# One PSUM bank in halves for sums that begin as a copy, and projection sums handed over one by one

## Chip, cores and metric

The kernel runs on one core of one Trainium2 chip. The metric is the device time of one execution in microseconds (us). The profile is one execution taken by the hardware profiler on the same core. Engines: PE (TensorE), DVE (VectorE), ACT (ScalarE), POOL (GpSimd) and SP (SyncE, which here only issues DMAs).

## The reference

With x of 3327 x 512, a 0/1 matrix adj of 3327 x 3327 (about 1% ones), two weights W of 512 x 1024 and one weight of 512 x 512, all float32:

```
h = x
for W in W_stack:                       # two layers
    Wh, Ws = split(h @ W, 2, axis=-1)   # two of 3327 x 512
    a = softmax(Wh @ Ws.T, axis=-1) * adj
    h = leaky_relu(a @ Wh + h, 0.01)
x = layernorm(x + h)
xw = maximum(sign(x), 0) @ sign(weight).T
return layernorm(x + relu(adj @ xw))
```

## The kernel before

**Tiling.** The 3327 rows are 26 tiles of 128. Four tiles make a chunk (seven chunks c, the last of two tiles), two tiles a pair (13 pairs q as keys, 13 column halves g as queries). A product `A @ B` whose operands split into 2 x 2 blocks is made in seven block products (r 1 to 7) in place of eight, from sums of the blocks; four of these at once (a quad of two pairs q, against both halves g of a chunk) are made in 26 products in place of 28. All of it is float32, 128 x 128 weights against 256 columns; a matmul of this kind shows as two records.

**The projection** (`project`, once per layer) makes Wh for each pair (`project_values`) and the query forms for each chunk (`queries`, names ending in `_g`). Each is a chain of seven products (`seven`, from line 199): three sums Z, Y, X, each in a PSUM bank, where X begins as a copy of Z by ACT (`seeded`) and gets only product 2. The sums of operands that a chain needs (`left_sums`, `right_sums`: `key_sums`, the `sums` of `queries`) and those made from its results (`done`, `last_sums`, and `query_sums` for the blocks' extra forms `ge`) are DVE work; POOL's queue stores the results to DRAM (`xs_d`, `ws_d`, `gs_d`, `ge_d`). `weave` lists the steps of several chains by their relative places, and everything is issued in that order (a manual schedule), so each engine runs its part of one written order.

**The attention** (`attention`, once per layer) goes through 169 steps (g, q): softmax weights times adjacency times Wh, as seven-product chains into the `acc` banks (L1092). Woven into the steps are the scores of the chunk ahead, 26 half-steps u for each chunk, of some 6 us each. A pair q outside the quads gets one chain by `scores`: z1, y5, z6, y3 in the first half-step, z7, x2, z4 in the second (L771), sums Z, Y, X. A quad (four in layer 1, three in layer 2) gets one block by `quad_scores` in four half-steps (L811): 26 products in the order

```
ORDER = (11, 8, 3, 23, 14, 16, 12, 22, 9, 1, 25, 20, 4,
         21, 13, 7, 19, 24, 6, 5, 15, 18, 2, 10, 17, 0)
```

into the sums P, Q, R, S, T. There are 49 blocks. A running sum is read out along the way, by ACT (`keep_as`, L817) or by a DVE addition (`out`, L823); at two places ACT copies a kept value into a bank to go on from there (`seed`, L820): u2 into Q before r19, c30 into P before r17. The work of a half-step is a list of pairs (place, operation), sorted by place.

**Loads.** Query forms of a chunk (`ga`, `gb`; seven forms B11, T1, T2, B22, T3, B21, T4) are loaded on SP's queue by `load_gs` (L748): five of them in half-steps 20 to 24 of the chunk before, the last two (B21, read by x2, and T4, read by z4) in half-step 0 of the chunk itself. Where a chunk has a single buffer for a form, SP waits for the last reader.

**Column maximum.** For the softmax, `column_max` folds each half's running maximum; in `across`, seven copies of 32 partitions by ACT bring the partial maxima together and spread the result.

**PSUM** has eight banks: three in the pool `ps_ch` (tag `ch`: the sums Z, X, Y of chains and P, Q, R, S, T of blocks), four in `ps_acc`, one in `ps_tr`. In the projection the chains of values use `acc`, those of queries `ch`. `copied` (L885) keeps u2 and p5 of a chain.

Of the kernel before, what the change touches and what calls it, by code (L numbers as in the profile page):

```python
# [19 lines left out]
P = 128  # L20
# [25 lines left out]
def kernel(  # L46
# [39 lines left out]
    ps_ch = ctx.enter_context(tc.tile_pool(name="ps_ch", bufs=3, space=PSUM))  # L86
# [10 lines left out]
    with tc.manual_schedule():  # L97
        make_identity(nc, ident)
        drum = keep.tile([P, HW], BF16, name="drum")
        nc.vector.memset(drum, 0.0)  # L100

        def beat(lane, times):
            pool, tag = lane
            t = pool.tile([P, HW], F32, tag=tag, name="beat")
            for _ in range(times):
                nc.tensor.matmul(t, drum[:, :P], drum, start=True, stop=True)

        for n in range(3):
            beat((ps_ch, "ch"), 2)
        for n in range(4):  # L110
            beat((ps_acc, "acc"), 2 - n % 2)
# [92 lines left out]
    def seven(lane, name, multiply, c11, c12, c21, c22):  # L204
# [19 lines left out]
        def seeded():  # L224
            bank["X"] = pool.tile([P, HW], F32, tag=tag, name=f"pX_{name}")
            nc.scalar.copy(bank["X"], bank["Z"])
# [15 lines left out]
    def left_sums(a11, a12, a21, a22, s1, s2, s3, s4, eng=nc.vector, between=lambda: None):  # L242
        eng.tensor_tensor(s1, a21, a22, ALU.add)
        eng.tensor_tensor(s2, s1, a11, ALU.subtract)
        between()
        eng.tensor_tensor(s3, a11, a21, ALU.subtract)
        eng.tensor_tensor(s4, a12, s2, ALU.subtract)

    def right_sums(b11, b12, b21, b22, t1, t2, t3, t4):
        nc.vector.tensor_tensor(t1, b12, b11, ALU.subtract)  # L250
        nc.vector.tensor_tensor(t2, b22, t1, ALU.subtract)
        nc.vector.tensor_tensor(t3, b22, b12, ALU.subtract)
        nc.vector.tensor_tensor(t4, b21, t2, ALU.subtract)

    def weave(*lists):

        at = [
            ((i + 0.5) / len(part), n, do)
            for n, part in enumerate(lists) for i, do in enumerate(part)
        ]  # L260
        for _, _, do in sorted(at, key=lambda e: e[:2]):
            do()
# [12 lines left out]
    def key_sums(l, q, a, xT, between=lambda: None):  # L275
# [9 lines left out]
        left_sums(  # L285
            *(of[i] for i in (A11, A12, A21, A22, S1, S2, S3, S4)), between=between
        )
        return of
# [74 lines left out]
    def query_sums(l, c, gs, b12):  # L363
# [12 lines left out]
        def first():  # L376
            sub(23, gs[B11][:, 0], gs[T3][:, 1])
            sub(22, gs[B21][:, 1], gs[T4][:, 0])
            sub(2, gs[T3][:, 1], b12[:, 0])
            sub(5, at[22], gs[B22][:, 1])  # L380
            sub(3, at[22], gs[T3][:, 0])
            store(0, 4)

        def second():
            sub(7, gs[B22][:, 0], gs[T1][:, 1])
            sub(13, at[7], gs[B21][:, 0])
            sub(21, at[23], gs[T4][:, 1])
            sub(20, at[7], gs[B11][:, 1])
            sub(9, at[21], at[13])
            store(1, 2, 3)  # L390

        return [first, second]
# [70 lines left out]
    def project(l, pre):  # L463
# [32 lines left out]

        def transpose_x(c, a):
            if a == 0:
                xTs[c] = pre.tile([P, KD, CW], F32, tag="xT", bufs=2, name=f"xT_{l}_{c}")
# [5 lines left out]
        else:  # L505
            xTs[0] = x_first[l]
            for n in range(3):
                beat(ch_lane, 1)
# [28 lines left out]
        def keys(c, a, between=lambda: None):  # L537

            q = c * CT // 2 + a
            of = keys_first.pop((l, q), None) or key_sums(l, q, a, xTs[c], between)  # L540
            if q // 2 in QUADS[l]:
                return of
            to = xs_d[l][q]
            for raw in (A11, A12, A22):
                nc.gpsimd.dma_start(out=to[:, raw], in_=of[raw])
            nc.gpsimd.dma_start(out=to[:, S1 : S2 + 1], in_=of["s12"])
            nc.gpsimd.dma_start(out=to[:, S4 : S3 + 1], in_=of["s34"])
            return of

        def project_values(c, a, lane, between=lambda: None):  # L550
# [12 lines left out]
            def done():  # L563
                t12 = slot([P, 2, HD], F32, f"t12_{l}_{q}")
                t34 = slot([P, 2, HD], F32, f"t34_{l}_{q}")
                right_sums(b11, b12, b21, b22, t12[:, 0], t12[:, 1], t34[:, 0], t34[:, 1])
                nc.gpsimd.dma_start(out=ws_d[l][q][:, 0:2], in_=t12)
                nc.gpsimd.dma_start(out=ws_d[l][q][:, 2:4], in_=t34)

            of_pair[q] = of  # L570
            return (
                [lambda: of.update(keys(c, a, between))]
                + seven(lane, f"wh_{l}_{q}", multiply, b11, b12, b21, b22) + [done]
            )

        def queries(c, lanes):
# [15 lines left out]
            if len(halves_of(c)) == 1:  # L592
# [9 lines left out]
                def last_sums():  # L602
                    store(B11, B21, B22)
                    right_sums(gs[B11], lo[:, :, P:], *(gs[i] for i in (B21, B22, T1, T2, T3, T4)))
                    store(T1, T2, T3, T4)

                more = query_sums(l, c, gs, lo[:, :, P:])
                return None, [lambda e=e: one(e) for e in range(KD)] + [last_sums] + more, []
# [7 lines left out]
            def sums():  # L616
                right_sums(xr[B11], lo[:, :, HW:], *(xr[i] for i in (B21, B22, T1, T2, T3, T4)))
# [10 lines left out]
            def done():  # L628
                store(B11, B21, B22)
                right_sums(gs[B11], b12, *(gs[i] for i in (B21, B22, T1, T2, T3, T4)))  # L630
                store(T1, T2, T3, T4)

# [5 lines left out]
            more_of[c] = [done] + query_sums(l, c, gs, b12)  # L638
            return sums, one, two

        def sums_m():
            of = left(*m_of[l])
            left_sums(
                *(of[i] for i in (A11, A12, A21, A22, S1, S2, S3, S4)),
                eng=nc.gpsimd if l else nc.vector,
            )
# [6 lines left out]
        def prepare(c):  # L653
            start, *chains[c] = queries(c, (ch_lane, ch_lane if c else acc_lane))
            if start:
                start()

        if l == 0:

            first = project_values(0, 0, ch_lane, lambda: (parts[0](), parts[1]()))  # L660
            second = project_values(0, 1, ch_lane)
            first.pop(0)()
            for do in parts[2:]:
                do()
            turns = [lambda k=k: transpose_w(l, 0, k, tr_lane) for k in range(KD)]
            turns.insert(2, lambda: transpose_first(acc_lane, 1))
            turns += [second.pop(0), lambda: None]
            turns += [lambda k=k: transpose_w(l, 1, k, tr_lane) for k in range(KD)]
            for do in first + second[:3]:
                do()  # L670
                turns.pop(0)()
            second = second[3:]
            for do in turns:
                do()
            weave(product_m(l, acc_lane), second, [lambda: prepare(0)])
            sums_m()
        else:
            first, second = (
                project_values(0, a, lane) for a, lane in enumerate((ch_lane, acc_lane))
            )  # L680
            sums_m()
            weave(first, second, [lambda: prepare(0)])
        for c in range(NC):
            turns = []
            if c + 1 < NC:
                turns = [
                    lambda a=a: transpose_x(c + 1, a) for a in range(len(tiles_of(c + 1)))
                ]
                pairs_of[c + 1] = [
                    project_values(c + 1, a, acc_lane)  # L690
                    for a in range(2 if c + 1 in QUADS[l] else 1)
                ]
                turns += [part.pop(0) for part in pairs_of[c + 1]]
                turns += [lambda: prepare(c + 1)]
            turns = rest + turns
            rest = more_of.pop(c, [])
# [4 lines left out]
            else:  # L701
                one, two = chains[c]
                pairs = sum(pairs_of[c], [])
                for a in range(len(pairs_of[c]), len(tiles_of(c)) // 2):
                    pairs += project_values(c, a, acc_lane)
                rest.append(pairs.pop())
                quad = []
                if c in QUADS[l]:
                    quad = quad_sums(l, c, of_pair[2 * c], of_pair[2 * c + 1])
                weave(one + two, pairs, turns, quad)  # L710
        for do in rest:
            do()
# [10 lines left out]
    def attention(l, att):  # L723
# [52 lines left out]
        def quad_scores(c, i):  # L776
# [14 lines left out]
            def fresh(n):  # L791
# [3 lines left out]
            begins = {11: "P", 8: "Q", 3: "R", 24: "S", 10: "T"}  # L795
            joins = dict(zip(
                (23, 12, 1, 4, 7, 6, 18, 17, 14, 22, 25, 21, 19, 5, 2, 16, 9, 20, 13, 15, 0),
                "PPPPPPPPQQQQQQQRRRRST",
            ))

# [32 lines left out]
            for r, b, name, other in (  # L833
                (16, "R", "c10", "c10"), (12, "P", "c31", "c31"), (9, "R", "c11", "c11"),
                (21, "Q", "c10", "c10"), (7, "P", "c00", "c00"), (24, "S", "u3", "u3"),
                (6, "P", "c01", "c01"), (5, "Q", "c01", "c01"), (15, "S", "c20", "c20"),
                (18, "P", "c21", "c21"), (2, "Q", "c11", "c11"), (10, "T", "c21", "c21"),
                (17, "P", "c30", "u3"), (0, "T", "c31", "c31"),
# [5 lines left out]
                (2.42, lambda: seed("Q", "u2")),  # L844
                (3.65, lambda: seed("P", "c30")),
# [23 lines left out]
        def scores(c, q, s):  # L869
# [17 lines left out]
            def z1():  # L887
                product(c, q, "Z", A11, B11, True)
                ch["X"] = ps_ch.tile([P, w], F32, tag="ch", name=f"pX_{l}_{c}_{q}")
# [45 lines left out]
        def column_max(g):  # L935
# [18 lines left out]
            def across():  # L954
                for a in range(P // B):
                    nc.scalar.copy(quad[:B, a], part[ts(a, B)])
# [3 lines left out]
                for a in range(1, P // B):  # L960
                    nc.scalar.copy(whole[ts(a, B)], whole[:B])
# [264 lines left out]
        else:  # L1226
# [35 lines left out]
            def keys_of_first(a):  # L1262
                keys_first[l + 1, a] = key_sums(l + 1, a, a, x_first[l + 1])
# [23 lines left out]
        for v in range(-LOOK - 4, len(steps)):  # L1287
# [18 lines left out]
            if 0 < c < NC and i == 0:  # L1306
                load_gs(c, 5, 2)
            if 0 <= c < NC and 1 <= i < 6:
                load_ge(c, i - 1)
            work, after = after, []  # L1310
            if 0 <= v + 3 < len(steps):
# [82 lines left out]
    def aggregate(g, p, a, e):  # L1394

        if (p, a, e) == (0, 0, 0):
            pool, tag = tr_lane if g == 3 else ch_lane
# [278 lines left out]
```

## Time and profile before

| | |
|---|---|
| median of 3 runs | 2548.84 us (2544.43 to 2550.69) |
| profiled execution | 2545.21 us, span 2543.4 us |
| granted PE clock | 0.998 |
| busy: PE, DVE, POOL, ACT | 2487.9, 2024.7, 1432.6, 859.0 us |
| chain that ended last, by engine | PE 84%, DVE 8%, DMA 4%, issue 2% |
| value products (L1092), four groups | 402.3, 376.4, 376.3, 201.2 us |
| DMA | 652.15 MB, 256 GB/s over the span |

The span is the time from the first to the last recorded instruction. Layer 1 ends near 1223 us; the projections lie at about 30 to 190 and 1230 to 1395 us, the last part (aggregation) follows layer 2. Matmuls are pipelined, so a busy PE is not a PE at its peak, and a matmul's lateness is best read from the distance of starts. "x2" at the end of a timeline row is the number of records in it.

### The profile page before, as it was taken

How to read it: one execution, taken by the hardware profiler on the slowest of the kernel's cores; microseconds unless marked ns; L12 is line 12 of the kernel's file. 1: busy time of each engine (PE TensorE's matmuls, PEld its weight loads, DVE VectorE, ACT ScalarE, POOL GpSimd, SP SyncE). 2: the span in 40 equal slices, each digit the busy share in tenths (PEclk: the TensorE clock that was granted, in tenths of full speed). 3: DMA queues.
4: the chain of work that ended last, by engine and by line, in shares of the span. 5: the costliest groups of instructions: out<-in, count | busy, mean ns of one | idle time of the engine just before them, and what ended most of it. 6: DMA issues, size and time to landing. Idle time of an engine off the chain costs nothing.

```text
span 2543.4 us, 39247 instructions
## 1 busy us (share of the span) xinstructions
PE 2487.9 (98%) x12056; PEld 2137.9 (84%) x12056; DVE 2024.7 (80%) x4020; ACT 859.0 (34%) x2171; POOL 1432.6 (56%) x2452
## 2 busy tenths in 40 slices
PE   9999999999999999999999999999999999999998
PEld 7886888888888888888888788888888888888886
DVE  6976787888878888778897668788787887878876
ACT  3323433323333333322232343332323323332234
POOL 3873465666666665545586345566555665555531
PEclk9999999999999999999999999999999999999999
DMA  5876867777677776798778686877777777788985
GB/s 187 282 286 217 276 229 261 246 259 262 228 269 243 251 267 233 264 312 261 231 275 299 239 282 224 276 241 268 260 227 275 242 266 254 235 271 291 313 279 174
DMA packets 313957, 652.15 MB, mean 256 GB/s; under 512 B 35373, under 2 KB 170661, under 8 KB 313742
## 3 DMA queue, kind: packets, MB, share of 16 engines
q1 hardware_dynamic: 279022, 539.75, 63.4%
q0 software_dynamic: 34720, 109.84, 11.6%
q8 instruction: 98, 1.61, 0.3%
q14 instruction: 117, 0.96, 0.1%
HBM read 539.15 MB, written 110.29 MB: 255 GB/s over the span
## 4 chain that ended last, share of the span: by engine, by line
PE 84%; DVE 8%; DMA 4%; issue 2%; SPq 1%; ACT 1%; POOL 0%; DVEq 0%; ACTq 0%; POOLq 0%
PE acc L1092 36%; PE pZ L771 9%; PE pP L811 6%; PE pQ L811 6%; PE pY L771 4%; PE pR L811 4%; PE agg L1404 3%; DMA ga<-gs_d 3%; PE pX L771 3%; PE pZ_wh L558 2%; PE pZ_g L622 2%; PE pT L811 2%; PE pS L811 2%; DVE ge L370 1%; PE pY_wh L558 1%
## 5 line engine op out<-in xcount | busy, mean ns | idle before, releaser
L1065 POOL TENSOR_TENSOR as<-s 128x128 f32<-128x128 f32 x338 | 204.8, 606 | 675.5 <-DVE s L1032 555.7
L1092 PE MATMUL acc<-ws,s 128*128 128x256 f32 x1352 | 402.3, 379 | 0.0
L1022 ACT ACTIVATE s<-s 128x512 f32<-128x512 f32 x338 | 213.3, 631 | 506.4 <-DVE s L1016 505.4
L1092 PE MATMUL acc<-ws,as 128*128 128x256 f32 x1352 | 376.4, 379 | 0.0
L1092 PE MATMUL acc<-wh,s 128*128 128x256 f32 x1352 | 376.3, 379 | 0.0
L1045 POOL TENSOR_TENSOR deg<-deg,adj 128x256 fp8e4<-128x256 fp8e4 x338 | 248.4, 735 | 62.0 <-DMA adj<-in_adjT_dram 47.7
L1092 PEld LDWEIGHTS acc<-ws,as 128*128 128x128 f32 x1352 | 249.4, 190 | 35.3 <-issue 3.8
L1092 PEld LDWEIGHTS acc<-wh,s 128*128 128x128 f32 x1352 | 250.6, 190 | 32.6
L1092 PEld LDWEIGHTS acc<-ws,s 128*128 128x128 f32 x1352 | 250.8, 190 | 30.8
L1032 DVE TENSOR_TENSOR s<-s,adj 128x512 f32<-128x512 f32 x338 | 242.9, 719 | 9.2 <-DMA adj<-in_adjT_dram 3.4
L867 DVE TENSOR_TENSOR top<-top,s 128x512 f32<-128x512 f32 x286 | 230.4, 807 | 16.1 <-ACT s L918 13.6
L1027 DVE TENSOR_TENSOR total<-total,s 128x512 f32<-128x512 f32 x312 | 243.2, 779 | 0.0
L1016 DVE TENSOR_TENSOR s<-s,beside 128x512 f32<-128x512 f32 x338 | 228.6, 676 | 13.1 <-ACT beside L1011 13.0
L771 PE MATMUL pZ<-ga,xs 128*128 128x256 f32 (+1 forms) x912 | 213.2, 358 | 3.2 <-DVE s L910 2.6
L1066 POOL TENSOR_TENSOR s<-s 128x128 f32<-128x128 f32 x338 | 198.3, 587 | 27.0
L1092 PE MATMUL acc<-wh,as 128*128 128x256 f32 x676 | 201.2, 379 | 0.0
L1067 POOL TENSOR_TENSOR as<-s 128x128 f32<-128x128 f32 x338 | 185.4, 549 | 26.5
L1068 POOL TENSOR_TENSOR as<-s,as 128x128 f32<-128x128 f32 x338 | 180.1, 533 | 26.5
L771 PEld LDWEIGHTS pZ<-ga,xs 128*128 128x128 f32 x912 | 165.2, 190 | 26.5 <-DVE s L910 4.3
L817 ACT COPY s<-pP 128x256 f32<-128x256 f32 (+1 forms) x196 | 70.0, 357 | 248.9 <-PE pP L811 194.2
L811 PE MATMUL pP<-ga,xs 128*128 128x256 f32 (+1 forms) x518 | 144.9, 361 | 3.6 <-DMA xs<-xq_d 2.7
L1092 PEld LDWEIGHTS acc<-wh,as 128*128 128x128 f32 x676 | 123.1, 190 | 19.1 <-issue 3.3
(271 smaller groups left out, 4947.5 us busy)
## 6 DMA issues: line engine op xcount, KB each, us to landing
ws<-ws_d SPq DMA_DIRECT2D x338, 512.0 KB
adj<-in_adjT_dram SPq DMA_DIRECT2D x351, 256.0 KB
xs<-xq_d SPq DMA_DIRECT2D x98, 832.0 KB
xs<-xs_d SPq DMA_DIRECT2D x84, 512.0 KB
xs<-xs_d SPq DMA_DIRECT2D x84, 384.0 KB
gs_d<-gsp POOLq DMA_DIRECT2D x84, 256.0 KB, 4.6
ge_d<-ge POOLq DMA_DIRECT2D x60, 256.0 KB, 3.0
ga<-gs_d SPq DMA_DIRECT2D x54, 256.0 KB
```

The costliest lines, as they stand in the source:

```text
L771: nc.tensor.matmul(ch[bank], xs[c, q, a][:, k], query(c, b)[:, k], start=(start and k == 0), stop=(k == 1), skip_group_check=True,)
L811: nc.tensor.matmul(bank[b], xs[c, i, f"x{r}"], right, start=r in begins, stop=True, skip_group_check=True,)
L867: nc.vector.tensor_tensor(top[i], top[i], t, ALU.max)
L1016: nc.vector.tensor_tensor(s, s, at.to_broadcast([P, 2, HW]), ALU.subtract)
L1022: nc.scalar.activation(sc[g, q], sc[g, q], AF.Exp)
L1027: nc.vector.tensor_tensor(total[g], total[g], sc[g, q], ALU.add)
L1032: nc.vector.tensor_tensor(s, s, adj[g, q], ALU.mult)
L1045: nc.gpsimd.tensor_tensor(deg[:, g], deg[:, g], adj[g, q][:, a], ALU.add, saturate=False)
L1065: nc.gpsimd.tensor_tensor(s3, a11, a21, ALU.subtract)
L1066: nc.gpsimd.tensor_tensor(a21, a21, a22, ALU.add)
L1067: nc.gpsimd.tensor_tensor(s2, a21, a11, ALU.subtract)
L1092: nc.tensor.matmul(acc[g][i // 2][:, i % 2], a[i], b[i], start=(q == 0 and i % 2 == 0), stop=(q == NQ - 1), skip_group_check=True,)
```

## The change

- PSUM: `ps_ch` gets two banks in place of three. The third becomes a bank of its own, `side`, one tile of two halves of 256 columns, for the sums that begin as a copy or as zeros. The X sum of a chain in the projection goes to half 0 for chains of `ch_lane` and to half 1 for the others; X of a chain of scores goes to half q mod 2.
- Blocks: R goes to half 0 and is set to zero by DVE at the start of the block; it begins with r3 as before. What went on in Q from u2 (r19, r5, r2) becomes U in half 1, seeded at place 1.75 in place of 2.42. What went on in P from c30 (r17) becomes V in half 0, seeded at 2.7 in place of 3.65. P, Q, S, T use the two banks of `ps_ch`.
- Projection: the groups of four sums are handed to `weave` as single operations, with the stores between them; the sums after the last chain of a chunk go over into the next chunk's lists, those after its first chain get places of their own (0.53 and on, by 0.09).
- The loads of B21 and T4 of a chunk are issued in half-step 25 of the chunk before, at 0.43 and 0.8.
- In `across`, the copies for the first two halves g are made by DVE.
- Three warm-up matmuls at the start of layer 2 go, and one of the last part's sums uses `side`'s bank.

The diff, cut to its core:

```diff
-    ps_ch = ctx.enter_context(tc.tile_pool(name="ps_ch", bufs=3, space=PSUM))
+    ps_ch = ctx.enter_context(tc.tile_pool(name="ps_ch", bufs=2, space=PSUM))
+    ps_x = ctx.enter_context(tc.tile_pool(name="ps_x", bufs=1, space=PSUM))
...
+        side = ps_x.tile([P, 2, HW], F32, tag="x", name="side")
...
         def seeded():
-            bank["X"] = pool.tile([P, HW], F32, tag=tag, name=f"pX_{name}")
+            bank["X"] = side[:, 0 if lane == ch_lane else 1]
             nc.scalar.copy(bank["X"], bank["Z"])
...
+    def sums_by(eng, *of):
+        return [
+            lambda to=to, a=a, b=b, op=op: eng.tensor_tensor(to, a, b, op) for to, a, b, op in of
+        ]
...
     def weave(*lists):
         at = [
-            ((i + 0.5) / len(part), n, do)
+            ((i + 0.5) / len(part), n, do) if callable(do) else (do[0], n, do[1])
             for n, part in enumerate(lists) for i, do in enumerate(part)
         ]
...
-                rest.append(pairs.pop())
-                quad = []
+                pairs = pairs_of[c]
+                quad, sums = [], []
                 if c in QUADS[l]:
                     quad = quad_sums(l, c, of_pair[2 * c], of_pair[2 * c + 1])
-                weave(one + two, pairs, turns, quad)
+                if len(pairs) == 2:
+                    sums = [(0.53 + 0.09 * n, do) for n, do in enumerate(pairs[0][2])]
+                rest = pairs[-1][2] + rest
+                weave(one + two, sum((part[1] for part in pairs), []), turns, quad, sums)
...
-            begins = {11: "P", 8: "Q", 3: "R", 24: "S", 10: "T"}
+            begins = {11: "P", 8: "Q", 24: "S", 10: "T"}
             joins = dict(zip(
-                (23, 12, 1, 4, 7, 6, 18, 17, 14, 22, 25, 21, 19, 5, 2, 16, 9, 20, 13, 15, 0),
-                "PPPPPPPPQQQQQQQRRRRST",
+                (23, 12, 1, 4, 7, 6, 18, 14, 22, 25, 21, 3, 16, 9, 20, 13, 19, 5, 2, 17, 15, 0),
+                "PPPPPPPQQQQRRRRRUUUVST",
             ))
+            bank.update({n: side[:, e, :w] for n, e in (("R", 0), ("V", 0), ("U", 1))})
...
-                (2.42, lambda: seed("Q", "u2")),
-                (3.65, lambda: seed("P", "c30")),
+                (0.0, lambda: nc.vector.memset(bank["R"], 0.0)),
+                (1.75, lambda: seed("U", "u2")),
+                (2.7, lambda: seed("V", "c30")),
...
             def z1():
                 product(c, q, "Z", A11, B11, True)
-                ch["X"] = ps_ch.tile([P, w], F32, tag="ch", name=f"pX_{l}_{c}_{q}")
+                ch["X"] = side[:, q % 2, :w]
                 nc.scalar.copy(ch["X"], ch["Z"])
...
             def across():
+                copy = nc.vector.tensor_copy if g < 2 else nc.scalar.copy
                 for a in range(P // B):
-                    nc.scalar.copy(quad[:B, a], part[ts(a, B)])
+                    copy(quad[:B, a], part[ts(a, B)])
...
-            if 0 < c < NC and i == 0:
-                load_gs(c, 5, 2)
...
+            if 0 <= c < NC - 1 and i == 2 * NQ - 1:
+                work += [
+                    (at, lambda c=c, n=n: load_gs(c + 1, n)) for n, at in ((5, 0.43), (6, 0.8))
+                ]
```

## The prediction

> **What bounds the kernel now.** I read the page's busy shares first, then the waits of TensorE (PE), then the timelines around the places that the change touches, then the windows of the projection.
>
> ```profile
> PE 2487.9 (98%) x12056; PEld 2137.9 (84%) x12056; DVE 2024.7 (80%) x4020; ACT 859.0 (34%) x2171; POOL 1432.6 (56%) x2452
> ```
>
> PE is the bound: all that can be won is what PE idles, all that can be lost is a new wait of PE, which takes its work in program order. The matmul count does not change (three warm-up beats, 0.3 us, go). Start to start, records follow each other at 0.216 us (128x256); summed over the timeline, PE's starts are some 72 us late against that pace. Columns: waited for, us in total, times, longest.
>
> ```profile
> PE pX L771 <- DMA ga<-gs_d: 7.4, 9, 1.7
> PE pZ_wh L558 <- DVE wh L222: 6.7, 7, 2.2
> PE pQ L811 <- ACT pQ L820: 4.7, 10, 1.6
> PE pZ L771 <- ACT u L885: 3.9, 4, 1.7
> PE pZ_g L622 <- DVE gsp L222: 2.6, 3, 0.9
> PE pS L811 <- DVE qu L823: 2.3, 5, 0.8
> ```
>
> Below, for how soon PE can follow a ScalarE (ACT) seed: the last column's brackets hold idle time and its releaser.
>
> ```profile
> 1841.40 0.37 ACT L817 COPY s<-pP 128x256 f32<-128x256 f32 x1 [1.41 <-PE pP L811]
> 1841.67 0.62 ACT L1040 CAST ab<-adj 128x512 fp8e4<-128x512 f32 x1
> 1842.21 0.37 ACT L817 COPY qu<-pQ 128x256 f32<-128x256 f32 x1
> ...
> 1847.12 0.35 ACT L817 COPY s<-pR 128x256 f32<-128x256 f32 x1
> 1847.37 0.38 ACT L820 COPY pQ<-qu 128x256 f32<-128x256 f32 x1
> ```
>
> ```profile
> 1841.58 0.59 PE L811 MATMUL pQ<-ga,xs 128*128 128x256 f32 x2
> 1842.01 0.59 PE L1092 MATMUL acc<-ws,s 128*128 128x256 f32 x2
> 1842.44 0.59 PE L811 MATMUL pR<-ga,xs 128*128 128x256 f32 x2
> ...
> 1847.80 0.70 PE L811 MATMUL pQ<-gb,xs 128*128 128x256 f32 x2 [0.45 <-ACT pQ L820]
> ```
>
> Four constants come from these. A product's second record starts 0.22 after its first (1841.58, 1841.79); the copy of its bank starts 0.42 after that (1842.21). A next ACT operation starts 0.25 to 0.27 after a copy's start. A copy lasts 0.37, and PE starts 0.05 after a seed's end (1847.75, 1847.80). A matmul that waited shows 0.70 instead of 0.59: 0.1 more is lost at its second record.
>
> **The change, part by part.** *Halves of one bank.* The built program of the changed kernel keeps its semaphores by whole tile, and `side` is one tile of two halves, so an operation on one half waits for the operations on the other. Two waits are new that way.
>
> First, blocks. r20 (R, half 0) waits for the seed of U (half 1), which now stands in ACT's order right behind the copy of u3 out of r25's bank. The rows above are this place: r25 at 1841.58, copy at 1842.21, r20 at 1842.44. The seed would run from 1842.48 to 1842.85, r20 start at 1842.90: 0.47 late with the rounding, plus 0.10. Of the 49 blocks, 30 have this spacing: 17.1 us. Five have three matmuls between (0.87 instead of 0.65 after r25's second record: 0.35 each, 1.8); six of half width cost 0.36, one 0.15 (2.3 together); seven have no matmul between, two at 1.0 and five at 1.36 (8.8). Sum 30. What follows r20 moves with it, so this lies on PE's path whole, unless a later wait of the same block shrinks.
>
> Second, projection. Two chains run woven, and their X sums get one half each. The second chain's x2 comes right behind the first's, and must now wait until ACT has copied the first one's X out:
>
> ```profile
> 83.81 1.03 PE L558 MATMUL pX_wh<-wa,xT 128*128 128x256 f32 x4
> 84.67 1.03 PE L622 MATMUL pX_g<-xT,m 128*128 128x256 f32 x4
> 85.86 1.13 PE L558 MATMUL pZ_wh<-wsum,xT 128*128 128x256 f32 x4 [0.15 <-DVE wh L222]
> ```
>
> ```profile
> 84.88 0.37 ACT L234 COPY wh<-pX_wh 128x256 f32<-128x256 f32 x1 [3.94 <-PE pX_wh L558]
> ```
>
> That copy ends at 85.25, so the x2 at 84.67 starts at 85.30: 0.63, and 0.10 at its second record. The order has 23 such pairs: 16.8 us. No row of before has two sums in the halves of one bank that two engines take turns on, so the bounds of both waits are nothing (if the wait is met by something else) and the price above; I take the price, since every term is a row.
>
> The Trainium skill, "PSUM — Partial Sum Buffer", section "PSUM bank collisions raise a hardware error", speaks against this part: no two engines may touch one bank at once, disjoint columns included, so guards go by bank and not by address. By it the waits are needed and stay; a chip that let halves go their own ways would make the sum 47 us less. The rows of before can't tell, for the same reason.
>
> Third, smaller. P, Q, S, T now share two banks, so r8 (second of a block) waits for DVE's last sum of the block before; in the trace there is a second of slack (1.0 us) except in five early blocks: 5 x 0.3, 1.7 us. The 49 new memsets of R go to DVE; none of that shape in PSUM is in the trace, so between nothing and the 0.34 pitch of a DVE 128x256 sum. DVE (80% busy) hides them but in five blocks where it runs without a gap, at most 1.7 us; I take nothing, since r3 starts 0.4 behind r8. New losses: 48.5 us.
>
> What the part wins: U's seed is placed 0.67 of a step (some 4 us) sooner, ahead of its first product r19. r19's waits (4.7 in the waits, 8.2 by late starts) mostly go: the rest, from ACT standing behind a late exponential (1846.58 in this block), may stay. I take 4.5.
>
> *Late forms.* B21 and T4 of the next chunk (L748) are loaded behind step 0's other loads, though the last reader is done earlier.
>
> ```profile
> 423.82 0.92 SPq L748 DMA_DIRECT2D ga<-gs_d  x2
> ...
> 430.95 1.13 PE L771 MATMUL pX<-ga,xs 128*128 128x256 f32 x4 [0.83 <-DMA ga<-gs_d]
> ```
>
> (The first line is SP's queue, the second PE's timeline.) Issue to use is 7.1 us, the use 0.83 late. The last reader of B21 ends at 418.9 and of T4 at 421.1, so the two loads can go 4.9 and 3.1 us sooner; both are then there in time. SP waits for these readers with nothing behind it until the next step's loads, which start 0.9 us later than now, four steps (adj) and two (ws, xs) ahead of use. Ten of twelve chunk starts are late, 10.2 us with the second records: gain 10.
>
> *Single sums in the projection.*
>
> ```profile
> 60.00:100.00 40.00, 38.09 (x174) 32.42 (x173) 36.57 (x68) 13.60 (x41) 33.44 (x65) 1.00 0.90 307
> 100.00:140.00 40.00, 36.88 (x169) 31.34 (x168) 38.04 (x72) 13.15 (x40) 31.71 (x62) 1.00 0.69 252
> ```
>
> (Busy us in order PE, weight load, DVE.) DVE has 2 to 3.4 us free of 40: its work just fits, and the waits come from groups of sums that run in one piece before the add that PE needs (pZ_wh and pZ_g wait for L222). Eleven such places (61, 86, 88, 112, 114, 140; 1243, 1268, 1293, 1295, 1320) cost 12.9 us by late starts, 9.3 of it in the waits; handed over singly, an add waits for one 0.34 us sum and not for four. Of 12.9 I leave 2.4, as DVE stays nearly full: gain 10.5. The sums put off past each projection's end make its attention start wait (2.3 us per layer); fewer are put off: gain 3.6 of 4.6. A slot that POOL's store reads is written again 4.8 us after the store in layer 1, with a landing of 4.0: no cost, but little room.
>
> *Column maximum.* For g below 2 the seven small copies go from ACT to DVE. z7 waits for ACT's u2 copy behind them (3.9 us in four waits above, 5.1 with the second records and z4). DVE then carries them, at most 7 x 0.2 each, and the adds that release z4 stand behind them: gain 2.5, between nothing and 5.
>
> Lateness that r20's wait gives DVE to catch up with (r15 4.4 us and r0 6.4 us of late starts, both on DVE): I take 1.5 of 10.8.
>
> Gains: 10 + 10.5 + 3.6 + 4.5 + 2.5 + 1.5 + 0.3 = 32.9. Losses 48.5. Net 15.6 later: 2545.2 becomes 2560.8 for the profiled execution. The median of the runs lies 3.6 above the profiled one, so 2564.4, or 2564.
>
> **Rivals.** *The new waits are absorbed.* If r20's wait frees DVE and ACT so that the late starts of r15, r0, r17 and r19 all go (4.4 + 6.4 + 2.6 + 8.2 = 21.6 instead of 6), the net is 0: 2549. For it: all four waits are on DVE or ACT, which lag and don't lead. Against it: most of this lateness is in few blocks, and in the others 0.57 meets nothing to absorb. Range 2542 to 2556.
>
> *Faster: the halves don't wait for each other.* Then the 46.8 us are gone: 2564 - 47 = 2517. It decides as soon as the seed of U ends before r20's natural start, 0.65 us after r25's second record, or ACT's copy within the 0.2 us between two x2. With the block's wait alone hidden the net is -14: 2534; with the projection's alone, 2547. Against it: the semaphores in the program. For it: only that prices come from one place each.
>
> *Worse: DVE.* The memsets (49 x 0.34, 16.7 us) and the max copies come on top of an engine at 92% to 95% in the projection and full in some blocks. If a third of the blocks pay the memset (5.6), and the single sums bring half (5.3 less), the time is 2575.
>
> **Numbers.** The main case 0.66, by itself 2556 to 2573; absorbed 0.15; halves apart, in whole or part, 0.14; worse 0.05. The range leaves out the full form of the second rival and the far end of the last: 2534 to 2578. This kernel's measurement tells about 0.3% from no change, 7.6 us, so faster is below 2541.2 and slower above 2556.5. Faster: the halves apart, and a little of the absorbed, 0.16. Same: most of the absorbed, and an edge of the main case, 0.14. Slower 0.70.
>
> **What will show it.** In the waits of PE after: pR <- ACT on the U seed, about 49 times and 25 us, and pX_wh or pX_g in the projection <- ACT L234's copy, 23 times and 14 us, are the two claims; either one missing makes the forecast wrong by its term. pX <- DMA ga should be gone, pZ_wh and pZ_g <- DVE under 3 us together, pQ <- ACT seed replaced by pU under 4. The ACT timeline should show u3's copy, the U seed 0.27 later, and r20 0.05 after its end. If DVE's busy share in 60 to 140 rises above 96%, or pQ <- DVE appears in most blocks, the last rival is at work.

## Result and the profile after

The changed kernel takes 2575.78 us (median of 4 runs, 2573.93 to 2576.47) against 2547.86 us before (4 runs): a ratio of 1.0109, 95% interval 1.0092 to 1.0127. It is 27.9 us slower; the forecast was 2564, in the range 2534 to 2578. The profiled execution's span went from 2543.4 to 2574.0 us, 30.6 more.

PE's busy share first, then the longest waits of PE after the change (waited for, us in total, times, longest):

```profile
PE 2501.4 (97%) x12053; PEld 2137.1 (83%) x12053; DVE 2033.9 (79%) x4097; ACT 855.1 (33%) x2143; POOL 1435.3 (56%) x2452
```

```profile
PE side L814 <- ACT side L823: 16.7, 38, 1.1
PE side L814 <- DVE side L847: 13.1, 13, 1.5
PE side L566 <- ACT gsp L240: 10.3, 20, 0.6
PE pZ L773 <- DVE s L914: 4.1, 5, 1.3
PE pZ_g L631 <- DVE gsp L228: 3.0, 3, 1.4
PE pS L814 <- DVE qu L826: 1.9, 4, 0.6
```

Three waits on `side` head the list, and none of them was there before. The wait of pX on ga is gone, and so is pZ_wh on DVE. The first and the third are the two waits that the prediction names; the second, on L847, the memset of R, it had priced at nothing.

The place of the forecast, r20 behind U's seed, in a block of layer 1 (ACT's timeline, then PE's):

```profile
308.14 0.37 ACT L820 COPY qu<-pQ 128x256 f32<-128x256 f32 x1
308.41 0.38 ACT L823 COPY side<-qu 128x256 f32<-128x256 f32 x1
```

```profile
307.94 0.59 PE L1097 MATMUL acc<-ws,s 128*128 128x256 f32 x2
308.85 0.70 PE L814 MATMUL side<-ga,xs 128*128 128x256 f32 x2 [0.31 <-ACT side L823]
```

Copy of u3, 0.27 later the seed, 0.06 after its end r20: it starts 0.91 after the product in front of it in place of 0.43, so 0.48 late, and 0.10 more at the second record (0.70 for 0.59). The bracket shows 0.31, counted from the modelled end of the product in front; start to start the lateness is larger, and that is what adds up to the span.

The second wait, two X in the projection (PE, then ACT):

```profile
85.81 1.03 PE L631 MATMUL side<-xT,m 128*128 128x256 f32 x4
87.34 1.13 PE L566 MATMUL side<-wa,xT 128*128 128x256 f32 x4 [0.51 <-ACT gsp L240]
```

```profile
86.92 0.37 ACT L240 COPY gsp<-side 128x256 f32<-128x256 f32 x1 [3.99 <-PE side L631]
```

The two products stand 1.53 apart in place of 0.86: 0.67 and 0.10.

The wait that the prediction missed, at the first block of a chunk (DVE, then PE):

```profile
455.31 0.41 DVE L1134 TENSOR_TENSOR h<-acc,ou 128x256 f32<-128x256 f32 x1
455.64 1.15 DVE L869 TENSOR_TENSOR top<-s,s 128x512 f32<-128x512 f32 x1
456.71 0.68 DVE L1021 TENSOR_TENSOR s<-s,beside 128x512 f32<-128x512 f32 x1
457.43 0.27 DVE L847 MEMSET side<- 128x256 f32 x1
```

```profile
457.76 0.70 PE L814 MATMUL side<-gb,xs 128*128 128x256 f32 x2 [0.91 <-DVE side L847]
```

The memset itself takes 0.27 us, as little as was thought. But DVE reaches it late, behind the sums that finish a column half (the last is the row at 455.31), a maximum of 1.15 us and one operation more, and r3 is 1.07 late and 0.10 at its second record. This happens at the first block of a chunk in 13 of the 14 chunks of the two layers, with 0.5 to 1.6 us at the first record.

Late starts of PE by product, start to start against the pace of 0.216 us (128x256), summed over the trace (the warm-up matmuls at its start, at half pace in every kernel, are not counted):

| us late | before | after | no_banks | by_cost |
|---|---|---|---|---|
| r20 | 0.2 | 30.7 | 0.3 | 0.3 |
| r3 | 0 | 16.6 | 0 | 0 |
| X of the projection | 0 | 18.0 | 0 | 0 |
| x2 at a chunk's start | 10.2 | 0 | 0 | 0 |
| Z and Y of the projection | 13.8 | 6.3 | 21.2 | 14.1 |
| r19, r17 | 10.7 | 6.0 | 10.7 | 10.7 |
| r15, r0 | 10.8 | 9.6 | 10.6 | 10.4 |
| r14, r21, r8 | 5.9 | 2.6 | 5.8 | 5.9 |
| z1, y3, z7, z4 | 10.8 | 6.6 | 6.6 | 5.8 |
| all, with products not listed | 70.9 | 102.2 | 60.4 | 51.7 |

The lateness grows by 31.3 us, the span by 30.6: the waits are the loss. (The last two columns are experiments, told below.)

### The profile page after: what moved, and what is told of

Read it like the earlier page. It is cut to its first block, busy times and chain, and to the rows that moved or that the text cites. A ratio compares the mean times of both kernels' runs of the same rounds, so it can differ in the third digit from the quotient of the medians.

```text
span 2574.0 us, 39238 instructions
## 1 busy us (share of the span) xinstructions
PE 2501.4 (97%) x12053; PEld 2137.1 (83%) x12053; DVE 2033.9 (79%) x4097; ACT 855.1 (33%) x2143; POOL 1435.3 (56%) x2452
## 4 chain that ended last, share of the span: by engine, by line
PE 87%; DVE 7%; ACT 2%; issue 2%; DMA 1%; POOL 0%; ACTq 0%; SPq 0%; DVEq 0%; POOLq 0%
PE acc L1097 36%; PE pZ L773 9%; PE side L814 7%; PE pP L814 5%; PE pY L773 5%; PE pZ_wh L566 3%; PE pZ_g L631 3%; PE pQ L814 3%; PE agg L1413 3%; PE side L773 2%; PE pY_wh L566 2%; PE pT L814 2%; PE pS L814 2%; PE pY_g L631 1%; PE pm L461 1%
## 5 line engine op out<-in xcount | busy, mean ns | idle before, releaser
L1050 POOL TENSOR_TENSOR deg<-deg,adj 128x256 fp8e4<-128x256 fp8e4 x338 | 241.8, 715 | 53.3 <-DMA adj<-in_adjT_dram 38.6
L814 PE MATMUL side<-ga,xs 128*128 128x256 f32 (+1 forms) x462 | 137.5, 379 | 13.9 <-DVE side L847 6.2
L1053 POOL DMA_DIRECT2D adj_d<-ab x169 | 94.2, 557 | 81.0 <-ACT ab L1045 51.2
```

Of the source, the lines that this page charges most:

```text
L814: nc.tensor.matmul(bank[b], xs[c, i, f"x{r}"], right, start=r in begins, stop=True, skip_group_check=True,)
L1050: nc.gpsimd.tensor_tensor(deg[:, g], deg[:, g], adj[g, q][:, a], ALU.add, saturate=False)
```

## Experiments

Two theories were told apart. One: sharing the bank makes waits that simply add to PE's time. The other: DVE and ACT are behind anyway, and a wait that is removed comes back at a later product.

**seed_early**, the changed kernel with U seeded at another place:

```diff
-                (1.75, lambda: seed("U", "u2")),
+                (1.32, lambda: seed("U", "u2")),
```

> The changed kernel with one place altered: U is seeded at 1.32 in place of 1.75, right behind r9, so that the seed lies between two products of R that are 2.4 us apart and not behind the copy of u3. Theory (an operation on one half of the shared bank waits for the other half, so r20 waits for the seed): r20's lateness, 30.7 us in 49 blocks, falls under 3, nothing else grows by over 3, and the time falls by 25 to 30 us, to about 2548. Rival (PE only waits at r20 for what it would wait for later, DVE and ACT being behind anyway): the lateness comes back at r19, r15, r0 or r8, and the time falls by less than 10.

Measured: 2560.06 us, ratio to before 1.0050 (1.0034 to 1.0065), 15.7 less than the changed kernel. r20's lateness fell from 30.7 to 2.8, as expected, but 12 us came back. 7 of them stand where the rival has them: r15 and r0 went from 9.6 to 13.3 in sum, r19 and r17 from 6.0 to 9.3. Two waits show it:

```profile
PE pS L814 <- DVE qu L826: 3.7, 7, 1.0
PE side L814 <- ACT s L820: 2.8, 5, 1.5
```

The other 5 us are not the rival's: r11 and r21 wait 1.7 us each more for their DMA, and the projection, which seeds no U, is 1.9 us later with 13 records at half pace in it (see the last section). Nothing here ties these to the seed; r11's lateness alone is 0.4 us in no_banks and 5.3 in loads_only. So both theories were half right: the wait is real and goes when the seed moves, over half of it is kept, and a quarter comes back at products that wait for DVE or ACT.

**proj_x_apart**, the changed kernel with the value chains' X in a bank of `acc` again:

```diff
-            bank["X"] = side[:, 0 if lane == ch_lane else 1]
+            bank["X"] = side[:, 0] if lane == ch_lane else pool.tile(
+                [P, HW], F32, tag=tag, name=f"pX_{name}"
+            )
```

> The changed kernel with X of the value chains of the projection (and of the second query chain in chunk 0) in a bank of its own from the pool acc, as before; X of the other chains stays in the half. Theory: the 23 places where the second chain's product 2 waits for ACT's copy of the first one's X go, 18.0 us by late starts, and the time falls by 16 to 18, to about 2558.5. Rival (the projection is bound by DVE, which is 90 to 95% busy in it, so PE's wait only gives DVE time): pZ_wh and pZ_g wait for DVE instead, 10 us or more are late there, and the time falls by under 8.

Measured: 2568.57 us, ratio 1.0088 (1.0072 to 1.0103), 7.2 less. The 18.0 us are gone, but Z and Y of the projection went from 6.3 to 17.4 us late:

```profile
PE pZ_g L633 <- DVE gsp L228: 13.1, 8, 2.9
```

Here the rival was right: 11 of the 18 us of X's waits had been time in which DVE caught up.

**zero_early**, the changed kernel with the first memset of a chunk in the half-step before:

```diff
-                (0.0, lambda: nc.vector.memset(bank["R"], 0.0)),
+                (0.0, lambda: None if i == quads[0] else nc.vector.memset(bank["R"], 0.0)),
...
-            ] + [(0.62, lambda i=i: maximum(i, q)) for i in mine[1:]]
+            ] + [(0.62, lambda i=i: maximum(i, q)) for i in mine[1:]] + [
+                (0.5, lambda: nc.vector.memset(side[:, 0, :w], 0.0))
+            ] * (q == 2 * quads[0] - 1)
```

> The changed kernel with the memset of R of the first block of each chunk moved half a half-step and more ahead, to place 0.5 of the half-step before (behind the copy of the preceding chain's X); the other 36 blocks as they are. Theory (the memset's cost is the queue that it stands in on DVE: after the sums that finish a column half and two maxima): r3's lateness, 16.6 us in 13 blocks, falls under 3, and the time falls by 13 to 16, to about 2561. Rival (DVE has no room there, whatever the order): the adds and outs behind the moved memset are late by as much, z4 and r8 or r15 take up 8 us or more, and the time falls by under 6.

Measured: 2562.59 us, ratio 1.0058 (1.0043 to 1.0074), 13.2 less. r3's 16.6 us fell to none, and 3.7 of them came back at r14, two products on. The price was the memset's place in the queue: the same memsets (14 are moved, one for each chunk; 13 had held PE up), issued earlier, cost a fifth.

**all_three** has the three edits together.

> The three alterations together: U seeded at 1.32, the value chains' X apart, the first memset of a chunk ahead. Theory (three separate costs of sharing the bank, that add up): late starts fall from 102 to about 38 us, the time to about 2515, 1.3% under the kernel before. Rival (DVE and ACT take back a good part): 2530 to 2545.

Measured: 2540.94 us, ratio 0.9980 (0.9971 to 0.9989): 34.8 less than the changed kernel. The single edits sum to 15.7 + 7.2 + 13.2 = 36.1, so they add up; what did not come, 26 of the 61 expected, is what each fell short of by itself. Late starts are 65.3 us in all, 17.9 of them Z and Y of the projection.

The parts one by one, in the kernel before. **loads_only** moves the two late loads:

```diff
-            if 0 < c < NC and i == 0:
-                load_gs(c, 5, 2)
...
+            if 0 <= c < NC - 1 and i == 2 * NQ - 1:
+                work += [
+                    (at, lambda c=c, n=n: load_gs(c + 1, n)) for n, at in ((5, 0.43), (6, 0.8))
+                ]
```

> The kernel before with the late form loads alone moved (B21 and T4 in half-step 25 of the chunk before). Theory (a load issued late is all that x2 waits for at a chunk's start): the waits of pX on ga go, 10.2 us by late starts, and nothing takes their place: 2537 to 2539, ratio 0.996. Rival (the sums behind x2 then wait for DVE): 2543 or more.

Measured: 2535.51 us against 2547.69, ratio 0.9950 (0.9937 to 0.9963). The 10.2 us of x2 are gone, and the median gains 12.2. The profiled execution, at 2540.35 the longest of the five, can't show that nothing took their place: its late starts are only some 5 us less than before, with 3.3 us more at Z and Y of the projection and 1.9 more at r11; 14 records at half pace (see the last section) are 3.0 us of all that came up.

**sums_only** has the single sums of the projection and the lists that carry them, with the three banks, the loads and the column maximum as before (its diff is that part of the change).

> The kernel before with the projection's sums handed over singly, and nothing else (three banks, as before). The prediction's step: pZ_wh and pZ_g late by 13.8 us before, 11 less after, and some 3 us at the start of each attention: 14 us gained, 2534. Rival (DVE is the bound of the projection; its sums take the same time in any order): pZ_wh and pZ_g stay 12 us or more late, 2 to 4 us are gained at the starts of the attention alone, 2544 to 2546.

Measured: 2545.20 us against 2547.69, ratio 0.9994 (0.9984 to 1.0003): no gain that can be told. The wait of pZ_wh is gone, that of pZ_g has taken its place (Z and Y together are 18.8 us late, 13.8 before), and one place shows how (PE's waits; DVE's timeline; PE's timeline):

```profile
PE pZ_g L627 <- DVE gsp L222: 12.9, 8, 2.9
```

```profile
117.71 2.10 DVE L278 STREAM_TRANSPOSE xT<-xr 128x512 f32<-128x512 f32 x2
119.75 0.37 DVE L244 TENSOR_TENSOR t<-wh,t 128x256 f32<-128x256 f32 x1
120.05 2.08 DVE L278 STREAM_TRANSPOSE xT<-xr 128x512 f32<-128x512 f32 x2
...
125.86 0.41 DVE L222 TENSOR_TENSOR gsp<-pZ_g,h_g 128x256 f32<-128x256 f32 x1
```

```profile
126.33 1.13 PE L627 MATMUL pZ_g<-xt,m 128*128 128x256 f32 x4 [2.94 <-DVE gsp L222]
```

Four transposes of 1.05 us and then the key sums follow each other, each given one equal step of the list. The addition that frees Z stands behind them, though single.

One more cause shows in the traces, and no run tests it by itself. In no_banks (told below) DVE is already late when it comes to these transposes, as a sum had to wait for its slot until a store of `gs` had landed, and DVE has no gap from there to the addition that PE waits for (DVE's timeline, then PE's):

```profile
118.09 0.57 DVE L244 TENSOR_TENSOR t<-wb,wh 128x256 f32<-128x256 f32 x1 [1.83 <-DMA gs_d<-gsp]
```

```profile
128.38 2.08 PE L627 MATMUL pZ_g<-xt,m 128*128 128x256 f32 x4 [2.91 <-DVE gsp L222]
```

The same happens there in layer 2 (2.33 us of DVE at 1317, 3.45 us of PE at 1327). In the projections before, DVE has no wait for a store. The prediction had put the slots at "no cost, but little room"; how much of the lateness at Z and Y is theirs is not shown.

**across_only** moves the column maximum's copies to DVE:

```diff
+                copy = nc.vector.tensor_copy if g < 2 else nc.scalar.copy
...
-                    nc.scalar.copy(quad[:B, a], part[ts(a, B)])
+                    copy(quad[:B, a], part[ts(a, B)])
...
-                    nc.scalar.copy(whole[ts(a, B)], whole[:B])
+                    copy(whole[ts(a, B)], whole[:B])
```

> The kernel before with the column maximum's copies for g below 2 on DVE, and nothing else. The prediction's step: z7 and z4 near 282 and 1485 wait 2.5 us less, 2545. Rival (the copies hold up DVE's adds there as they held up ACT's copy): the wait on ACT turns into one on DVE of the same size, within 1.5 us of no change.

Measured: 2546.70 us against 2547.69, ratio 0.9999 (0.9990 to 1.0008). z7's 3.9 us near 282 and 1485 are gone; the next product there is x2, which then waits for its late load instead (1.5 us at 283; pX's waits on ga are 12.8 us in twelve). With the loads moved, as in the changed kernel, z4 is 1.55 late there in both layers, on DVE's addition. The wait changed its engine.

**no_banks** is the changed kernel without the shared bank: loads, single sums and column maximum stay.

> The changed kernel with everything about the shared bank undone (three banks for the chains and blocks, R, Q and P as before, the warm-up matmuls as before); loads, single sums and column maximum as changed. Theory (the shared bank is the only part that loses): 2529 to 2534, so that the bank's parts cost some 43 us of the changed kernel's time. Rival (the single sums lose in the projection once PE doesn't wait for X there): 2536 to 2540.

Measured: 2535.83 us, ratio 0.9955 (0.9943 to 0.9967), the same as the moved loads alone and between the 2534 of the theory and the 2536 of the rival; Z and Y are 21.2 us late, so the single sums do lose in the projection, as the rival has it. So the shared bank costs 2575.78 - 2535.83 = 40.0 us of the changed kernel, and the other two parts bring nothing beside the loads. Freed of its three waits (all_three) it is still 5.1 us behind.

**by_cost** tests whether the projection's DVE is too full or only badly ordered: no_banks with the operations of a chunk placed by the time that each takes.

```diff
+    def cost(us, do):
+        do.us = us
+        return do
+
+    def by_cost(todo, later):
+        whole = sum(getattr(do, "us", 0.04) for do in todo)
+        half = 0.53 * (whole + later)
+        placed, at = [], 0.0
+        for do in todo:
+            us = getattr(do, "us", 0.04)
+            n = at + us / 2
+            placed.append((
+                0.53 * n / half if n < half else 0.53 + 0.47 * (n - half) / (whole - half), do
+            ))
+            at += us
+        return placed
...
-                weave(one + two, sum((part[1] for part in pairs), []), turns, quad, sums)
+                weave(one + two, sum((part[1] for part in pairs), []), by_cost(turns, 1.5 if sums else 0.0), quad, sums)
```

(Costs: 0.02 + 0.0013 us for each column of a sum, 0.5 for a difference of `query_sums`, 1.05 for a transpose.)

> As no_banks (three banks, late loads, single sums, column maximum), with the single sums, differences and transposes of a chunk placed by the DVE time that each takes (0.35, 0.5, 0.7, 1.05 us) in place of one equal step for each. Theory (pZ_g waits because DVE's queue piles up where long operations stand close together, four transposes and eight key sums in a row, while DVE idles early in the chunk waiting for pY_g): pZ_g and pZ_wh late by 20 us in no_banks fall to 6 to 10, and the time by 10, to about 2526. Rival (DVE's total, 92 to 95% of the projection, is the bound): the same lateness at other products, within 4 us of no_banks.

Measured: 2526.52 us, ratio 0.9920 (0.9905 to 0.9935), 9.3 less than no_banks. The windows of the projection (busy us of PE, weight load, DVE):

```profile
60.00:100.00 40.00, 39.83 (x185) 34.58 (x184) 39.63 (x73) 14.67 (x47) 34.52 (x64) 1.00 0.78 277
100.00:140.00 40.00, 38.93 (x180) 33.63 (x179) 39.09 (x72) 13.07 (x39) 34.85 (x65) 1.00 0.75 277
```

In the first window DVE is now 39.6 of 40 us busy and PE 39.8: DVE's work fits, and little is left there. Z and Y of the projection are still 14.1 us late. The longest waits, 5.9 us, are pY_g on ACT in three places; but ACT was not busy, it had itself waited 6.4 to 8.5 us for a store to land (ACT, then PE, at the longest):

```profile
1335.57 0.37 ACT L235 COPY gsp<-pZ_g 128x256 f32<-128x256 f32 x1 [6.36 <-DMA ws_d<-t]
```

```profile
1336.00 2.07 PE L648 MATMUL pY_g<-xt,msum 128*128 128x256 f32 x4 [3.74 <-ACT gsp L235]
```

**by_cost_seed** adds one thing, Q's seed ahead of the copy of c00:

```diff
-                (2.42, lambda: seed("Q", "u2")),
+                (2.18, lambda: seed("Q", "u2")),
```

> As by_cost, with the seed of u2 into Q at 2.18 in place of 2.42, ahead of the copy of c00 on ACT. r19 is late by 8 us in no_banks, as the seed stands behind that copy (0.27 us) and a late exponential. Theory: r19's lateness falls to 4 or 5 us and the time by 3 to 4 against by_cost. Rival (the seed then waits for DVE's out of r21 and holds ACT up): no gain, r15 or r0 later instead.

Measured: 2525.70 us, ratio 0.9915 (0.9899 to 0.9930). r19 went from 8.2 to 5.3 us late, r15 took 0.8 of it back; the time can't be told from by_cost. These two are the fastest versions, 0.8% under the kernel before and 1.9% under the changed one.

## Why the prediction was right, and where it was not

The direction and the range held, and the two waits that decided it were named with their place and price. But the sum was 15.6 us and the trace has 31, and 2575.8 lies above the 2556 to 2573 that the main case had by itself: the range held only by the room left for its rivals. Misses of 24 us against the forecast met 9 us of gains that the sum had not seen, which is luck. Four terms were off by most.

| term | forecast | in the trace after |
|---|---|---|
| r20 behind U's seed | +30.0 | +30.5 |
| second X in the projection | +16.8 | +18.0 |
| r8 behind the last sum | +1.7 | +2.6 |
| memset of R, r3 | 0 | +16.6 |
| late loads | -10 | -10.2 |
| single sums, projection | -10.5 | -7.5 |
| starts of the attention | -3.6 | -3.2 |
| column maximum | -2.5 | -1.0 |
| r19 | -4.5 | -4.9 |
| r15, r0 | -1.5 | -1.2 |
| r14, r21 | not seen | -5.9 |
| r11 and the rest | -0.3 | -2.5 |

- *The step that failed is the memset's.* "I take nothing, since r3 starts 0.4 behind r8" looked at r8 in a steady row of blocks (start to start r3 is 0.86 behind it in the trace of before). At the first block of a chunk DVE's queue holds the finishing sums and the maxima. What is to be looked up for an added operation is not its length (0.27 us) but how far its engine is behind at that place, in the trace of before. The last rival had the memset on DVE as its mechanism and 2575 as its time, at a chance of 0.05, though with a wrong spread: a third of the blocks at 0.34, where it was 13 blocks at 1.27. Its own signs did not show: DVE is busy 36.1 and 36.8 of 40 us in the two windows of 60 to 140 us (90% and 92%), and pQ waits for DVE twice.
- *The single sums were right in the trace and wrong in cause.* Z and Y gained 7.5 us after the change, but alone (sums_only) they lose 5.0, and in proj_x_apart 11 us of lateness come back there: PE's new waits at X had let DVE catch up. The step "an add waits for one 0.34 us sum and not for four" left out what else stands in the queue, transposes of 1.05 us in pairs, and the slots' stores. by_cost shows that the order was at fault, not DVE's total; whether by the pairs or by the stores is open.
- *The column maximum* had its gain and its loss in one sentence, and the loss was taken too small: the wait went to DVE.
- *r14 and r21* are late in the kernel before and were not in the sum; r3's wait covers r14's (it returns in zero_early). That is the mirror of the absorbed rival, which was right about places but not about size: without r20's wait 12 of 28 us come back (7 of them at DVE or ACT), without the X waits 11 of 18, without r3's 4 of 17.
- *The rule on banks.* By the Trainium skill, "PSUM — Partial Sum Buffer", section "PSUM bank collisions raise a hardware error", guards go by bank and not by address. The runs show what guards by whole tile, here one bank, cost: 0.58 and 0.77 us in the places shown. No run here has an engine on each half at once, so the chip's own part in it is not shown.

## What to carry over

Halving one bank between sums that different engines read and write at different times makes one queue of them, where the semaphores keep it whole, as here; put an operation on one half where the other half is quiet (U's seed in the 2.4 us between two products of R), or don't share. An operation added to an engine costs what that engine is behind at its place; and a gain measured beside a new stall may be the stall's own doing, so each part wants a run alone. Where several engines follow one written order, spread the operations by their length, not by their number.

## Not expected

- After a long wait PE came back at half pace for some products. In no_banks PE waited 2.91 us at 125 to 128 us, and the granted clock of the four us behind it, the column after POOL's, is 0.66:

```profile
129.00:133.00 4.00, 4.00 (x14) 3.31 (x13) 3.96 (x9) 0.78 (x3) 1.33 (x3) 0.66 0.93 368
```

  The waits of 3.45 us in no_banks, 3.74 in by_cost, 2.12 in seed_early (at 1338 us) and 2.14 in loads_only (at 1317) were followed by such products too; one of 2.94 us in sums_only, one of 3.23 in by_cost_seed and two of 2.9 in proj_x_apart were not. Each record at half pace is 0.21 us late, and 6 to 13 of them in a row cost 1.3 to 2.7 us. So a wait of 2 us or more may cost that much beside itself, and not always; what decides is not shown.
- The page's wait for r20 (16.7 us in 38) is little over half of its lateness (30.7 us): a wait is counted from the modelled end of the product in front, and the second record's 0.10 us is not in it.
